# A message-passing layer: sums and counts leave PSUM on ScalarE and go to two tables in DRAM, in place of adds on VectorE, and 48 feature columns a step are copied on chip in place of 40

## The chip, the cores and the metric

The kernel runs on one core of a Trainium2 chip. The metric is the device time of one execution in microseconds (us). Before the change it is 1895.83 us, the median of three runs (1894.88 to 1898.73).

A core has TensorE (PE: matmuls out of SBUF into PSUM), VectorE (DVE), ScalarE (ACT), GpSimd (POOL) and SyncE (SP), each with an instruction queue of its own, and 16 DMA engines that all queues share. SBUF and PSUM are the memories on the chip, of 128 partitions each; DRAM is off it.

## The reference, cut to what matters

`x` holds 12,500 nodes with 64 features. There are 212,500 edges with 32 features each, sorted by their destination, and every node has at least the edge from itself.

```
msg_in   = concat(x[src], x[dst], edge_attr)              # 160 values an edge
messages = relu(msg_in @ mW1 + mb1) @ mW2 + mb2           # 160 -> 128 -> 64
agg      = segment_sum(messages, dst)                     # one row a node
u        = relu(concat(x, agg) @ uW1 + ub1) @ uW2 + ub2   # 128 -> 128 -> 64
out      = layernorm(x + u)                               # over 64 values, no gain
```

The second message product is linear, so it can follow the sum. The kernel sums the 128 hidden values of a node's edges, counts the edges (for `mb2`), and multiplies the sums once by `wc` = mW2 @ uW1[64:].

## The kernel before

**Groups and steps.** The edges form 554 groups of `GE` = 384 (three tiles of 128). Since they are sorted, the destinations of a group lie in a window of `W` = 32 nodes. One step `k` of the main loop (lines 716 to 772) works on three groups at once: `turn` on group k, `hidden` on k-2, `sums` on k-4. In the last ten steps (`SHORT`) the three catch up with each other.

- `turn` (line 423): `own.s` holds an edge a row: 64 gathered source features, and a one-hot of 32 columns for its destination within the window, which VectorE writes (`onehot`, line 409). TensorE transposes the three tiles into PSUM, and ScalarE copies the result, 96 rows by 384, to `own.st` (line 440).
- `hidden` (line 448): one matmul a tile, of `own.st` (64 rows source features, 32 rows one-hot, 32 rows edge features that a DMA has put there) with `own.wm` (64 rows of mW1, the window's 32 rows of `by_dst`, which is x @ mW1[64:128] + mb1 in DRAM, and 32 rows of mW1). VectorE takes the relu to `own.h` (line 464).
- `sums` (line 474): one matmul a tile of the hidden values with the one-hot (the one-hot four times side by side, `TIMES`), 128 hidden by 32 nodes, and one of ones with the one-hot for the counts. VectorE adds the sums to `agg` (128 by nodes in SBUF, line 493) and the counts to row 96 of `xc` (line 494), at columns that come from a register which `places` has loaded.

**Where source features come from.** For most groups POOL gathers them: an indirect DMA a tile (line 184), 16 groups ahead, into a ring of 20. Beside that, the transposed features of all nodes lie in SBUF as `xc`. For the groups in `COPIED` there is no gather: VectorE (line 597) and ScalarE (line 599) copy single columns of `xc`, 64 partitions by four bytes, into `own.st`, at addresses that they load into registers first (line 576). From step `BEGIN` = 18 on, `COLS` = 40 columns go each step, 20 on each of the two engines, in parts of `VCOLS` and `ACOLS`. Once 384 are done another group is complete; 54 groups are copied in this way.

**The update of nodes.** Nodes go in 25 chunks of 512. A chunk is closed at a group whose number follows from the edges' count (`PLAN`); from then on one part of its update runs in each step (`step_update`, line 663): `inner` (two products of 512 columns), `relu`, `outer` (eight products), `stats`, `root`, `scaled` with the store of the output.

**Order.** Each engine runs its instructions in the order written. A step's matmuls wait once, at the first, for all that the step needs; PSUM has two slots for each of the three parts, so a step waits for the copies, relus and adds of two steps earlier. SP's queue holds in program order the window loads (`window`, line 390, four groups ahead), the edge features (`inputs`, line 355), the indices and the outputs. A second program, `unordered`, runs only if a test on the chip finds that the edges do not fit.

## Time and profile before

| what | value |
|---|---|
| median of three runs | 1895.83 us |
| the profiled execution | 1894.96 us, its span 1893.1 us |
| mean granted TensorE clock | 0.963 |
| busy: PE, DVE, ACT, POOL | 1336.2, 1475.6, 1385.6, 1418.0 us |
| indirect gathers on POOL | 1499, 945 ns each |
| column copies on ACT and on DVE | 10360 and 10376 |
| moved by DMA | 104.90 MB, 55 GB/s on average |

Busy time is time in which an engine executes; loads of registers, semaphore operations and the issue of DMAs do not count as busy. A row of a group reads: line, engine, operation, output and inputs, count, then busy time in all and mean ns of one, then the idle time of the engine just before such instructions and what ended most of it. The profile infers who ended a wait from semaphore events, so a name there can be wrong where several things had been waited for. Timelines give start and length in us from the start of the span; an fp32 matmul appears as two instructions.

### The profile page before, as it was taken

The page shows a single profiled execution, that of the slowest core. Times are in us where ns is not written, and L with a number is a line of the kernel's source. Part 1 is how long each engine was busy: PE and PEld are TensorE (multiplying, and loading weights), DVE is VectorE, ACT ScalarE, POOL GpSimd, SP SyncE. Part 2 cuts the span into 40 slices and gives each one's busy share as a digit, 9 for nine tenths or more (in the row PEclk, how much of TensorE's full clock was granted, in tenths as well). Part 3 has the DMA queues.
Part 4 walks back from the last instruction along what each step waited for, and adds up shares of the span by engine and source line. Part 5 has one row for each costly group of instructions (what it writes and reads, how often), then busy time and mean ns, then how long its engine had stood idle before and what let it go on. Part 6 is the DMA issues. An engine that isn't in the chain of part 4 may idle for free. (4 is left out here: it accounts for less than half of the span.)

```text
span 1893.1 us, 60001 instructions
## 1 busy us (share of the span) xinstructions
PE 1336.2 (71%) x12323; PEld 1182.5 (62%) x12323; DVE 1475.6 (78%) x13054; ACT 1385.6 (73%) x11008; POOL 1418.0 (75%) x1506
## 2 busy tenths in 40 slices
PE   5877777757667666777677766776766757666767
PEld 4766666656556555666566665666666656656666
DVE  4468898878878788778887887878878888788763
ACT  3368888877777777777787777777777877777741
POOL 7777777777777777777777777777777777777774
PEclk9789999999999999989998999999999999999998
DMA  5542222222222222222222222222222222222221
GB/s 144 138 98 64 54 51 53 48 51 48 45 53 53 46 52 48 50 49 50 49 53 46 52 45 53 53 46 53 48 51 48 48 51 53 45 54 48 50 48 28
DMA packets 113382, 104.90 MB, mean 55 GB/s; under 512 B 51873, under 2 KB 83246, under 8 KB 113006
## 3 DMA queue, kind: packets, MB, share of 16 engines
q0 software_dynamic: 47968, 49.19, 13.6%
q1 hardware_dynamic: 64194, 51.30, 10.0%
q14 instruction: 272, 2.23, 0.4%
q8 instruction: 104, 1.70, 0.4%
q10 hardware_dynamic: 844, 0.48, 0.1%
HBM read 91.19 MB, written 9.62 MB: 53 GB/s over the span
## 5 line engine op out<-in xcount | busy, mean ns | idle before, releaser
L184 POOL DMA_INDIRECT own_s<-in_x,src_sb x1499 | 1417.3, 945 | 457.9 <-DMA own_s<-in_x,src_sb 206.3
L599 ACT ACTIVATE own_st<-own_xc 64x4 uint8 x10360 | 1089.2, 191 | 66.7 <-issue 18.6
L597 DVE COPY own_st<-own_xc 64x4 uint8 x10376 | 894.5, 191 | 171.1 <-issue 146.9
L429 PE MATMUL own_ps<-own_ident,own_s 128*96 128x128 f32 x1661 | 292.4, 287 | 512.0 <-ACT own_st L599 230.9
L440 ACT ACTIVATE own_st<-own_ps 96x384 f32<-96x384 f32 (+1 forms) x554 | 267.3, 483 | 383.0 <-PE own_ps L486 341.6
L429 PEld LDWEIGHTS own_ps<-own_ident,own_s 128*96 128x96 f32 x1661 | 166.4, 130 | 572.8 <-ACT own_st L599 311.4
L481 PE MATMUL own_ps<-own_s,own_h 128*128 128x128 f32 x3322 | 483.7, 284 | 1.9 <-DVE own_h L464 1.3
L453 PE MATMUL own_ps<-own_wm,own_st 128*128 128x128 f32 x3322 | 479.9, 283 | 0.0
L481 PEld LDWEIGHTS own_ps<-own_s,own_h 128*128 128x128 f32 x3322 | 436.0, 200 | 3.8 <-DVE own_h L464 2.4
L464 DVE TENSOR_SCALAR own_h<-own_ps 128x384 f32<-128x384 f32 x553 | 303.1, 548 | 167.4 <-PE own_ps L486 152.3
L453 PEld LDWEIGHTS own_ps<-own_wm,own_st 128*128 128x128 f32 x3322 | 431.7, 198 | 1.4 <-issue 0.5
L486 PE MATMUL own_ps<-own_s,own_one 128*1 128x32 f32 x3322 | 190.0, 194 | 0.0
L486 PEld LDWEIGHTS own_ps<-own_s,own_one 128*1 128x1 f32 x3322 | 114.5, 84 | 70.1 <-issue 7.2
L412 DVE TENSOR_TENSOR own_s<-iota,dlc 128x96 f32<-128x96 f32 x554 | 135.7, 246 | 0.8
L494 DVE TENSOR_TENSOR own_xc<-own_ps,own_xc 1x32 f32 x554 | 102.0, 184 | 28.8 <-PE u_ps L505 11.0
L493 DVE TENSOR_TENSOR own_agg<-own_ps,own_agg 128x32 f32 x554 | 97.9, 177 | 18.1 <-PE own_ps L486 10.3
L383 PE MATMUL u_ps<-w1b,own_xc 65*128 65x128 f32 x196 | 33.9, 325 | 28.6 <-DMA own_xc<-in_xT 12.6
L383 PEld LDWEIGHTS u_ps<-w1b,own_xc 65*128 65x128 f32 x196 | 28.7, 225 | 31.3 <-issue 20.3
L517 PE MATMUL u_ps<-same,own_xc 65*128 65x64 f32 (+1 forms) x196 | 39.5, 284 | 0.5 <-ACT u L510 0.5
L386 ACT ACTIVATE t<-u_ps 128x512 f32<-128x512 f32 (+1 forms) x25 | 14.7, 587 | 33.4 <-DMA by_dst<-t 16.7
L519 PE MATMUL u_ps<-u,u 128*128 128x64 f32 (+1 forms) x196 | 38.3, 277 | 0.0
L517 PEld LDWEIGHTS u_ps<-same,own_xc 65*128 65x128 f32 (+1 forms) x196 | 29.9, 192 | 2.4 <-ACT u L510 0.8
(60 smaller groups left out, 262.1 us busy)
## 6 DMA issues: line engine op xcount, KB each, us to landing
own_st<-in_efT SPq DMA_DIRECT2D x138, 192.0 KB
own_s<-in_x,src_sb POOLq DMA_INDIRECT x1499
own_wm<-by_dst SPq DMA_DIRECT2D x554, 16.0 KB
by_dst<-t SPq DMA_DIRECT2D x24, 256.0 KB
out<-o SPq DMA_DIRECT2D x24, 128.0 KB
own_xc<-in_xT SPq DMA_DIRECT2D x12, 179.2 KB
index<-in_src_copied SPq DMA_DIRECT2D x64, 1.2 KB
dlc_i<-in_dst_cols SPq DMA_DIRECT2D x1, 807.0 KB
```

Source lines behind the costliest of these rows:

```text
L184: nc.gpsimd.indirect_dma_start(out=s[:p, j, :D], out_offset=None, in_=x[:, :], in_offset=bass.IndirectOffsetOnAxis(ap=src_sb[:p, g * TG + ...
L412: places_by[g] = nc.vector.tensor_tensor(own.s[g % RING][:, :, D:], iota.unsqueeze(1).to_broadcast([P, TG, W]), dlc[:, g * TG : (g + 1) * ...
L429: nc.tensor.transpose(xt[:, j * P : j * P + p], sides[g] if g in sides and j == TG - 1 else s[:p, j, :], ident[:p, :p])
L440: after(nc.scalar.activation(t[r, c : c + n], xt[r, :n], AF.Copy), step))]
L453: nc.tensor.matmul(pre[:p, j, :], t[:, c + j * P : c + j * P + p], wm[g % NW], start=True, stop=True)
L464: relu_by[g] = [nc.vector.tensor_scalar(h, pre, 0.0, None, ALU.max)]
L481: did.append(nc.tensor.matmul(sg, h[:p, j, :], s[:p, j, D:].unsqueeze(1).to_broadcast([p, TIMES, W]), start=j == 0, stop=j == len(sizes) - 1))
L486: did.append(nc.tensor.matmul(counted, own.one[:p], s[:p, j, D:], start=j == 0, stop=j == len(sizes) - 1))
L493: a = after(nc.vector.tensor_tensor(agg[:, at], sg[:, 0, :], agg[:, at], ALU.add), step)
L494: return [a, after(nc.vector.tensor_tensor(count, counted, count, ALU.add), step)]
L597: by[engine] = nc.vector.tensor_copy(o, x_at)
L599: by[engine] = nc.scalar.activation(o, x_at, AF.Copy)
```

## The change

- `sums` now has the one-hot as the weights and the hidden values as the moving operand: the result is 32 nodes by 128, the counts are one column beside it. They lie in the same PSUM tile as the transposes of the step, at rows 64 to 95 and columns 384 to 512. ScalarE's copy of a step takes them along: 513 columns instead of 384. The adds on VectorE, their register loads (`places`) and `agg` are gone.
- SP stores the 32 rows, with 32 rows of zeros behind them, from `own.st` to a table in DRAM, even groups to one and odd groups to the other, at the window's first node (`store`). In the same table a later group overwrites the zeros of an earlier one, and at most two groups, one of each table, share a node.
- The update of a chunk begins two steps later (`SETTLED`) and has twelve parts in place of six: `found` loads the chunk's rows of both tables, `settled` only lets a step pass, `counts` and `all_sums` transpose and add the two by matmuls with the identity, `count_moved` (ScalarE) and `moved` (VectorE) copy the results out of PSUM; `inner` has three products.
- `hidden` runs three steps behind `turn` instead of two, `sums` six instead of four.
- `VCOLS` and `ACOLS` have another part of four each: 48 columns a step. A column is copied as one float and no more as four bytes.
- The edge features of four groups are loaded as four pieces a row, as the sums' columns lie between them. The test on the chip also asks that windows start in rising order and that the zeros reach the next group of the same table. `unordered` takes other memory.

```diff
-NW = 2 * SB
-COUNT = 96
-NH = 3
+NW = 8
+SLOTS = 2
+TO_HIDDEN, TO_SUMS = 3, 6
+NH = TO_SUMS - TO_HIDDEN + 1
+PLACE = TG * P + 132
+ROW = H + 1
+STORED = 2 * W
...
-TIMES = 4
+SETTLED = 2
 BEGIN = 18
 CHECKED = 8
-VCOLS = (12, 8)
-ACOLS = (8, 4, 4, 4)
+VCOLS = (12, 8, 4)
+ACOLS = (8, 4, 4, 4, 4)
 COLS = sum(VCOLS + ACOLS)
...
-        self.ps = [[on(f"own_ps{i}{k}", P, 512, of=nc.psum_tensor) for k in range(3)]
-                   for i in range(2)]
+
+        self.ps = [on(f"own_ps{i}", P, 1024, of=nc.psum_tensor) for i in range(SLOTS)]
+        self.pre = [on(f"own_pre{i}", P, 512, of=nc.psum_tensor) for i in range(SLOTS)]
...
+    def zeroed():
+
+        for ps in own.ps:
+            nc.vector.memset(ps[:D, GE : GE + ROW], 0.0)
+        for t in own.st:
+            nc.vector.memset(
+                t[D + W :, :].rearrange("p (g c) -> p g c", g=SB)[:, :, GE : GE + ROW], 0.0)
+        for n in range(0, STORED, W):
+            nc.sync.dma_start(tables[1][n : n + W, :], own.st[0][D + W :, GE : GE + ROW])
...
+    tables = [dram.tile([NP + STORED, ROW], F32, name=f"by_node{i}") for i in range(2)]
...
-        efs_by[b] = nc.sync.dma_start(own.st[b % BLOCKS][D + W :, : c1 - c0], a["efT"][:, c0:c1])
-        after(efs_by[b], *([hidden_by[(b - BLOCKS + 1) * SB - 1]] if b >= BLOCKS else []))
+        t = own.st[b % BLOCKS][D + W :, :].rearrange("p (g c) -> p g c", g=SB)
+        n, rest_n = divmod(c1 - c0, GE)
+        efs_by[b] = [nc.sync.dma_start(
+            t[:, :n, :GE], a["efT"][:, c0 : c0 + n * GE].rearrange("p (g c) -> p g c", g=n))]
+        if rest_n:
+            efs_by[b].append(nc.sync.dma_start(t[:, n, :rest_n], a["efT"][:, c0 + n * GE : c1]))
+        for i in efs_by[b]:
+            after(i, *([hidden_by[(b - BLOCKS + 1) * SB - 1]] if b >= BLOCKS else []))
...
+            for i in range(n):
+                at, store_at[g + i] = (of_words(v[2 * i + j].with_bounds(
+                    min_val=0, max_val=4 * size * (N - 1))) for j, size in enumerate((H, ROW)))
+                rows_at[g + i] = at
...
+    def store(g):
+
+        t, c, _ = columns(g + TO_SUMS)
+        table = tables[g % 2].rearrange("n w -> (n w)").bitcast(U8)
+        store_by[g] = nc.sync.dma_start(
+            table[bass.ds(store_at.pop(g), 4 * STORED * ROW)].rearrange("(n b) -> n b", n=STORED),
+            t[D:, c + GE : c + GE + ROW].bitcast(U8))
+        tc.add_to_no_dep_group("features", store_by[g].ins)
...
+            if step in with_sums:
+                n = GE + ROW
             copies = [ordered_by_steps(
-                after(nc.scalar.activation(t[r, c : c + n], xt[r, :n], AF.Copy), step))]
+                after(nc.scalar.activation(t[r, c : c + n], ps[r, :n], AF.Copy), step))]
...
-        sg = ps[2][:, : TIMES * W].rearrange("p (t w) -> p t w", w=W)
-        counted = ps[2][0:1, TIMES * W :][:, :W]
+        found, counted = ps[D : D + W, GE : GE + H], ps[D : D + W, GE + H : GE + ROW]
         did = []
-        for j, p in enumerate(sizes):
-            did.append(nc.tensor.matmul(
-                sg, h[:p, j, :],
-                s[:p, j, D:].unsqueeze(1).to_broadcast([p, TIMES, W]),
-                start=j == 0, stop=j == len(sizes) - 1))
-        for j, p in enumerate(sizes):
-            did.append(nc.tensor.matmul(counted, own.one[:p], s[:p, j, D:],
-                                        start=j == 0, stop=j == len(sizes) - 1))
-
-        def add(step):
+        for out_ps, of in ((counted, lambda j, p: own.one[:p]), (found, lambda j, p: h[:p, j, :])):
+            for j, p in enumerate(sizes):
+                did.append(nc.tensor.matmul(out_ps, s[:p, j, D:], of(j, p), start=j == 0,
+                                            stop=j == len(sizes) - 1))
+        emptied = store_by.get(g - BLOCKS * SB)
+
+        def moved(step):
             sums_by[g] = step
-            at = bass.ds(starts.pop(g), W)
-            count = xc[COUNT : COUNT + 1, at]
-            a = after(nc.vector.tensor_tensor(agg[:, at], sg[:, 0, :], agg[:, at], ALU.add), step)
-            return [a, after(nc.vector.tensor_tensor(count, counted, count, ALU.add), step)]
-
-        return did, [*relu_by[g], *copy_by[g]], add
+            if step in with_sums:
+                return copy_by[g + TO_SUMS]
+            t, c, _ = columns(g + TO_SUMS)
+            r = slice(D, D + W)
+            return [after(nc.scalar.activation(t[r, c + GE : c + GE + ROW], ps[r, GE : GE + ROW],
+                                               AF.Copy), step)]
+
+        return did, [*relu_by[g], *copy_by[g], *([emptied] if emptied else [])], moved
 
     def update(base, p, n):
 
         rows, q = slice(base, base + p * n), p * n
 
-        def inner():
+        def found():
+            parts = [found_p.tile([P, 4, ROW], F32, name=f"found{i}") for i in range(2)]
+            for t, table in zip(parts, tables):
+                nc.sync.dma_start(t[:p, :n], table[rows, :].rearrange("(n p) w -> p n w", p=p))
+            return parts
+
+        def settled(parts):
+            return parts
+
+        def joined(parts, w, rows_out):
+            ps = ups.tile([H, CH], F32, name="u_ps")[:rows_out]
+            for k in range(n):
+                for i, t in enumerate(parts):
+                    nc.tensor.matmul(ps[:, k * p : (k + 1) * p], t[:p, k, w], ident[:p, :p],
+                                     start=i == 0, stop=i == 1)
+            return ps
+
+        def counts(parts):
+            return parts, joined(parts, slice(H, ROW), 1)
+
+        def count_moved(got):
+            parts, ps = got
+            count = up.tile([1, CH], F32, name="count")
+            nc.scalar.activation(count[:, :q], ps[:, :q], AF.Copy)
+            return parts, count
+
+        def all_sums(got):
+            parts, count = got
+            return joined(parts, slice(0, H), H), count
+
+        def moved(got):
+            ps, count = got
+            agg = up.tile([H, CH], F32, name="agg")
+            nc.vector.tensor_copy(agg[:, :q], ps[:, :q])
+            return agg, count
+
+        def inner(moved_to):
+            agg, count = moved_to
             u_ps = ups.tile([H, CH], F32, name="u_ps")
-            nc.tensor.matmul(u_ps[:, :q], wc, agg[:, rows], start=True, stop=False)
-            nc.tensor.matmul(u_ps[:, :q], ux, xc[: COUNT + 1, rows], start=False, stop=True)
+            nc.tensor.matmul(u_ps[:, :q], wc, agg[:, :q], start=True, stop=False)
+            nc.tensor.matmul(u_ps[:, :q], per_edge, count[:, :q], start=False, stop=False)
+            nc.tensor.matmul(u_ps[:, :q], ux, xc[: D + 1, rows], start=False, stop=True)
...
-        return [inner, relu, outer, stats, root, scaled]
+        return [found, settled, counts, count_moved, all_sums, moved, inner, relu, outer, stats, root, scaled]
...
-            o = t.bitcast(U8)[:D, 4 * (first_c + c) : 4 * (first_c + c + 1)]
-            x_at = xc_bytes[:D, bass.ds(at - own.at, 4)]
+            o = t[:D, first_c + c : first_c + c + 1]
+            x_at = xc_bytes[:D, bass.ds(at - own.at, 4)].bitcast(F32)
...
-        if not now and waiting and waiting[0][0] <= g:
+        if not now and waiting and waiting[0][0] + SETTLED <= g:
...
-            ps, old = own.ps[g % 2], users[part][g % 2]
+            slot = (g + ahead_of[part]) % SLOTS
+            ps, old = (own.pre if part is hidden else own.ps)[slot], users[part][slot]
...
+        if {turn, sums} <= {part for part, _ in work}:
+            with_sums.add(did[-1])
         for part, g, _, _, follow in parts:
-            users[part][g % 2] = follow(did[-1])
+            users[part][(g + ahead_of[part]) % SLOTS] = follow(did[-1])
+        unstored.extend(g for part, g in work if part is sums)
+
+    def stored():
+
+        while unstored:
+            store(unstored.pop(0))
...
-            if k + 2 < BITS:
-                zeroed(k + 2)
...
-        if k % SB == 1:
-            places(k // SB + 1)
         if k < G - SHORT:
-            step((turn, k), *([(hidden, k - 2)] if k > 1 else []),
-                 *([(sums, k - 4)] if k > 3 else []))
-            made, summed = max(0, k - 1), max(0, k - 3)
+            step((turn, k), *([(hidden, k - TO_HIDDEN)] if k >= TO_HIDDEN else []),
+                 *([(sums, k - TO_SUMS)] if k >= TO_SUMS else []))
+            made, summed = max(0, k + 1 - TO_HIDDEN), max(0, k + 1 - TO_SUMS)
...
+        stored()
...
-        step_update(G)
+        step_update(G + SETTLED)
+    return sums_by[G - 1]
```

## The prediction

> **What bounds the kernel now.** I read the page's busy table first, then the costliest groups, the waits of GpSimd (POOL), its timeline at both ends, and a table of stretches. Busy shares alone decide nothing: four engines stand between 71% and 78%.

> ```profile
> span 1893.1 us, 60001 instructions
> PE 1336.2 (71%) x12323; PEld 1182.5 (62%) x12323; DVE 1475.6 (78%) x13054; ACT 1385.6 (73%) x11008; POOL 1418.0 (75%) x1506
> ...
> L184 POOL DMA_INDIRECT own_s<-in_x,src_sb x1499 | 1417.3, 945 | 457.9 <-DMA own_s<-in_x,src_sb 206.3
> L599 ACT ACTIVATE own_st<-own_xc 64x4 uint8 x10360 | 1089.2, 191 | 66.7 <-issue 18.6
> L597 DVE COPY own_st<-own_xc 64x4 uint8 x10376 | 894.5, 191 | 171.1 <-issue 146.9
> ```

> The 458 us that POOL sits idle look like slack. Its waits and the two ends of its timeline say otherwise:

> ```profile
> POOL own_s L184 <- DMA own_s<-in_x,src_sb: 206.3, 677, 0.3
> POOL own_s L184 <- issue: 196.0, 643, 0.3
> POOL own_s L184 <- ACT own_st L599: 37.5, 123, 0.3
> ```
> ```profile
> 2.96 1.15 POOL L184 DMA_INDIRECT own_s<-in_x,src_sb  x1 [1.38 <-DMA src_sb<-in_src]
> ...
> 1874.65 0.94 POOL L184 DMA_INDIRECT own_s<-in_x,src_sb  x1 [0.30 <-issue]
> 1875.89 0.89 POOL L184 DMA_INDIRECT own_s<-in_x,src_sb  x1 [0.30 <-issue]
> ```

> Every idle piece is 0.3 us (206.3/677, 196.0/643), whatever name it carries, and none is longer. So a gather costs 0.945 + 0.305 = 1.25 us, always: (1875.89 - 2.96)/1498 = 1.2503 us from first to last. POOL never waits for anybody; it is full, and its last gather starts 17.2 us before the span's end. The other engines follow it, as the pace of TensorE's (PE's) transposes shows (line 429, three matmuls to a step; columns: stretch, length, PE busy and count, weight loads):

> ```profile
> 180.00:280.00 100.00, 17.16 (x102) 9.79 (x102) 1.00 0.23 53
> ...
> 600.00:1000.00 400.00, 62.54 (x356) 35.28 (x357) 0.97 0.23 51
> ```

> Early, while gathered groups are still in store, 102/3 = 34 steps take 100 us, 2.94 us each; later 356/3 = 118.7 steps take 400 us, 3.37 each, and POOL's own is 1499 x 1.2503/554 = 3.383. PE, ScalarE (ACT) and VectorE (DVE) could thus go some 13% faster than they are fed.

> **What the change takes from POOL.** A column-copied group needs no gather. 40 columns a step make 54 such groups, 48 make 65: with starts at step 18 the formula gives ceil(384(n+1)/48) steps more for each, up to group 538. Gathers: 1499 - 11 x 3 = 1466. Worth 33 x 1.2503 = **41.3 us**. POOL's need falls to 1466 x 1.2503/554 = 3.308 us a step.

> **Can the others follow at 3.308?** ScalarE is the one to ask. While it ran at its own speed:

> ```profile
> 187.58 2.09 ACT L599 ACTIVATE own_st<-own_xc 64x4 uint8 x20
> 188.41 0.83 PE L481 MATMUL own_ps<-own_s,own_h 128*128 128x128 f32 x6
> 189.57 0.47 ACT L440 ACTIVATE own_st<-own_ps 96x384 f32<-96x384 f32 x1
> 190.17 2.09 ACT L599 ACTIVATE own_st<-own_xc 64x4 uint8 x20
> 192.16 0.47 ACT L440 ACTIVATE own_st<-own_ps 96x384 f32<-96x384 f32 x1
> ```

> From copy to copy 192.16 - 189.57 = 2.59 us with 20 columns, one every (2.09 - 0.19)/19 = 0.10 us. Four more add 0.40. The copy out of PSUM grows from 384 to 513 columns; two rows give the price of a column:

> ```profile
> L386 ACT ACTIVATE t<-u_ps 128x512 f32<-128x512 f32 x24 | 14.3, 596 | 31.4 <-PE u_ps L383 16.3 <-DMA by_dst<-t 14.7
> L440 ACT ACTIVATE own_st<-own_ps 96x384 f32<-96x384 f32 x499 | 241.0, 483 | 369.3 <-PE own_ps L486 330.9 <-PE own_ps L429 25.2 <-issue 9.3
> ```

> (596 - 483)/128 x 129 = 114 ns, of which part lies under the register load that separates copy and first column already (0.60 us from 189.57 to 190.17); between 0 and 0.11 I take 0.05. Each chunk of the update (one in about 22 steps) adds a count copy of 512 columns, 0.6/22 = 0.03, to a relu and a root that were there (0.04). Together 3.1 us a step: below 3.308, by 6%. That margin is the thin place of the forecast.

> VectorE loses the two adds and gains four columns:

> ```profile
> L494 DVE TENSOR_TENSOR own_xc<-own_ps,own_xc 1x32 f32 x554 | 102.0, 184 | 28.8 <-PE u_ps L505 11.0
> L493 DVE TENSOR_TENSOR own_agg<-own_ps,own_agg 128x32 f32 x554 | 97.9, 177 | 18.1 <-PE own_ps L486 10.3
> ```

> -199.9 us against 2104 x 894.5/10376 = +181, and 25 copies of 512 columns out of PSUM, +15 at 0.6 each (ScalarE's row, DVE has none of this size): 1472 us, 2.66 a step. The register load of every fourth step for the adds goes too. Not a bound.

> PE keeps its six sum matmuls, with a 32-column weight in place of 128; no row has that form, so between -0.4 us a step (half of the 0.83 above) and 0; I take 0, as the long move of 128 columns stays. The update gets 392 more matmuls against the identity (eight a chunk for counts, eight for sums) at 0.83/3 = 0.277, and a third product: 392 x 0.277 + 25 x 1.0 = 134 us, or 0.24 a step on PE's 1336.2/554 = 2.41 busy. Hidden in mid-kernel.

> SyncE issues one more transfer a step, 64 rows of 516 bytes, and two table loads a chunk, 31 MB in all beside 105 MB moved now. Its store waits for ScalarE's copy of the same step; behind it stand the window loads (needed seven steps after the one that issues them), edge features and indices. The loads of a chunk wait for the last stores:

> ```profile
> SPq L402 <- DMA by_dst<-t: 49.2, 23, 3.7
> ```

> A load behind a write of DRAM waited 49.2/23 = 2.1 us here; such a wait once in 22 steps is covered by those seven. If that cover failed, 25 x 2.1 = 53 us would be the most it could cost PE. I take 0.

> **The end is where the change pays back.** Nothing covers what follows the last gather. These rows are the end of before:

> ```profile
> 1859.42 1.13 PE L504 MATMUL u_ps<-own_agg,wc 128*128 128x512 f32 x2
> 1860.38 1.02 PE L505 MATMUL u_ps<-own_xc,ux 97*128 97x512 f32 x2
> ...
> 1866.57 0.43 PE L517 MATMUL u_ps<-same,own_xc 65*128 65x64 f32 x2
> ...
> 1868.18 0.39 PE L519 MATMUL u_ps<-u,u 128*128 128x64 f32 x2
> ...
> 1869.81 0.22 DVE L526 BATCH_NORM_STATS2 stats<-u_ps 128x6 f32<-128x64 f32 x1
> ...
> 1871.06 0.18 DVE L527 BATCH_NORM_AGGREGATE mv<-stats 128x2 f32<-128x6 f32 x1
> ...
> 1873.19 0.28 ACT L533 ACTIVATE rstd<-mv,eps 128x4 f32<-128x4 f32 x1
> ...
> 1875.35 0.18 DVE L538 RECIPROCAL rstd<-rstd 128x4 f32<-128x4 f32 x1
> 1875.57 1.10 DVE L541 TENSOR_SCALAR o<-u_ps,mv,rstd 128x64 f32<-128x64 f32 x4
> 1876.69 0.41 SPq L546 DMA_DIRECT2D out<-o  x1
> ...
> 1882.78 0.62 PE L504 MATMUL u_ps<-own_agg,wc 128*128 128x212 f32 x2 [0.28 <-DVE own_agg L493]
> 1883.86 0.35 ACT L510 ACTIVATE u<-u_ps 128x212 f32<-128x212 f32 x1 [4.81 <-PE u_ps L505]
> ```

> The last chunk but one ran its six parts beside the last steps, from 1859.42 to 1876.69; the last chunk began at 1882.78, after the last sums. Now a chunk has twelve parts, one for each sums step, and begins two steps later. By the plan's closing groups (546 for the last but one) it begins at sums 548; when sums 553 are done six parts are over, and inner, relu, outer, stats, root and scaled follow with nothing beside them. Only then, in program order on SyncE behind that chunk's output, come the last chunk's loads. New on the path, in us:
> - its joined sums (8 x 0.277 = 2.2) between the last steps on PE, and its counts two steps ahead, mostly in PE's idle time: 2.5 (0 to 4);
> - inner 3.0 (1859.42 to 1861.40 is 2.0 for two products, a third of 512 columns 1.0); relu 0.7 (596 ns and the handover); outer 2.0 (1866.57 to 1868.57); stats 1.5 (1869.81 to 1871.24); root 0.4; reciprocal and scaled 1.4; the output's issue 0.5: 9.5;
> - two loads, the second issued 0.4 later and landing 2.1 after: 2.5. For a load's landing the nearest is the index load that the first gather waits for, issued at 0.81 and followed by the gather at 2.96; twice that is the upper bound;
> - counts of the last chunk (4 x 0.277 and handovers, 1.2), their copy 0.4, sums 1.2, their copy 0.5: 3.3;
> - the third product of its inner part 0.5.

> ```profile
> 0.81 0.42 SPq L151 DMA_DIRECT2D src_sb<-in_src  x1
> ```

> Sum **18.3 us**, between 14 and 24. The last store (0.3 copy, issue, 2.1) ends under the 9.5 and costs nothing; without that cover it would cost 3. From the last relu on nothing changes.

> **Sum.** The profiled execution took 1894.96 us, 1.86 more than its span, and stands 0.9 under the median of the runs, 1895.83. 1894.96 - 41.3 + 18.3 = 1872.0.

> **The rivals.**
> *ScalarE becomes the bound* (the slower side). Its margin is 0.2 us a step; a column at 0.11 instead of 0.10, the whole 0.11 of the copy and a wait for late steps would use it up. For it: the 2.94 of the early stretch is 0.35 over the clean 2.59. Against it: part of that 0.35 were VectorE's register loads for the adds, which go. Copying lasts some 520 steps; at 3.40 a step it falls 520 x 0.092 = 48 us behind POOL, and the last 15 steps without copies, at about 2.6 against 3.75 for three gathers, give back 17: about 1872 + 31 = 1903. From about 3.38 a step on the gain is gone.

> *VectorE's copies hold POOL up.* The column copies turn from four bytes into one float. A long conversion did slow a gather:

> ```profile
> 22.01 1.00 DVE L263 CAST dlc<-dlc_i 128x1614 f32<-128x1614 int32 x1 [8.66 <-DMA dlc_i<-in_dst_cols]
> ...
> 22.39 1.44 POOL L184 DMA_INDIRECT own_s<-in_x,src_sb  x1 [0.30 <-issue]
> ```

> 1.44 instead of 0.94. But 10376 short copies beside 1499 gathers left their mean at 945 ns. A delay of 22.9/1466 = 0.016 us in every gather cancels the gain; 0.04 gives 1872 + 59 = 1931.
> [...]

> *The end stays as short as it was*: the chunks' new parts find room earlier, and the whole 41.3 comes through, 1853.7. The code's order speaks against it.

> **How the numbers follow.** Forecast 0.79, ScalarE 0.10, VectorE's copies 0.06, short end 0.05. The likeliest case's own range is 1894.96 - 41.3 + 14 to + 24, 1867 to 1878. The range for all reaches to 1862 and 1886: it takes in a lag of a few us that ScalarE has not made good when the copies end, and an end 5 us shorter than my lower bound. About 0.2% of this kernel, 3.8 us, can be told from no change. Faster: 0.79 + 0.05 = 0.84; the two slow cases give 0.05 to no change (a pace near 3.38, or a delay near 0.016) and 0.11 to slower.

> **What would show it.** 1466 gathers 1.25 us apart with idle pieces of 0.3 each, the last starting near 1834.6; ScalarE's group of column copies at 12480 and its busy time near 1685 (1385.6 + 2120 x 0.105 + 554 x 0.114 + 25 x 0.6); transposes at 2.94 to 3.2 us a step until about step 200 and 3.3 after; from the last gather's start to the span's end 35 us in place of 17.2, with the last chunk but one entirely behind the last sums. Wrong it would be if POOL's gathers show pieces over 0.3 that wait for ScalarE's copies, if their mean leaves 945 ns, or if transposes stay above 3.31 a step.

## The result and the profile after

The changed kernel takes **1879.83 us** (median of four runs, 1878.41 to 1880.89) where the kernel before takes 1895.36 beside it: a ratio of 0.9916, 95% interval 0.9899 to 0.9933. It is 15.5 us faster; 23.8 were forecast (1895.83 - 1872.0). The profiled execution took 1878.41 us, 1.72 more than its span of 1876.69.

The page of the changed kernel: span, busy time of each engine, then the three costliest groups.

```profile
span 1876.7 us, 66058 instructions
PE 1495.1 (80%) x13157; PEld 1217.2 (65%) x13157; DVE 1362.5 (73%) x14069; ACT 1619.6 (86%) x13169; POOL 1385.6 (74%) x1473
...
L193 POOL DMA_INDIRECT own_rows<-in_x,src_sb x1466 | 1384.8, 945 | 447.9 <-issue 178.6
L668 ACT ACTIVATE own_operands<-own_xc 64x1 f32 x12480 | 1295.1, 189 | 28.4 <-issue 6.7
L666 DVE COPY own_operands<-own_xc 64x1 f32 x12480 | 893.7, 136 | 283.4 <-issue 177.5
```

ScalarE is now the busiest engine, 86%. Whether it is the bound is read from POOL's waits (total, times, longest) and from the last gathers:

```profile
POOL own_rows L193 <- issue: 178.6, 586, 0.3
POOL own_rows L193 <- DMA own_rows<-in_x,src_sb: 132.3, 434, 0.3
POOL own_rows L193 <- ACT own_operands L668: 92.3, 303, 0.3
```

```profile
1832.13 0.95 POOL L193 DMA_INDIRECT own_rows<-in_x,src_sb  x1 [0.30 <-issue]
1833.38 0.90 POOL L193 DMA_INDIRECT own_rows<-in_x,src_sb  x1 [0.30 <-DMA own_rows<-in_x,src_sb]
```

Behind the first gather, which waits for its indices, no piece is over 0.3 us, whoever is named, as before. POOL is still full: 33 gathers fewer, and the last starts 42.5 us earlier (1875.89 to 1833.38). The pace of TensorE's transposes (three a step; stretch, length, TensorE's busy time and count, weight loads, granted clock) shows the other engines catching up and then following:

```profile
200.00:400.00 200.00, 33.73 (x195) 19.46 (x195) 0.98 0.34 71
400.00:600.00 200.00, 34.68 (x200) 19.41 (x198) 0.98 0.34 71
...
1400.00:1800.00 400.00, 65.62 (x366) 36.98 (x365) 0.94 0.33 68
```

65 steps in 200 us are 3.08 us each, then 3.0, and 3.28 at the end (366/3 = 122 steps in 400 us) where only POOL sets the pace: while columns are copied, one group in eight needs no gather (48/384), and 2.625 gathers a step at 1.25 us are 3.28. So at 48 columns the engines can go at about 3.05 and are fed at 3.28.

Of the 42.5 us, 26.05 come back behind the last gather: span minus its start is 1876.69 - 1833.38 = 43.31, against 1893.15 - 1875.89 = 17.26 before. The timeline of the end:

```profile
1842.32 1.13 PE L572 MATMUL u_ps<-agg,wc 128*128 128x512 f32 x2
...
1851.43 0.40 SPq L615 DMA_DIRECT2D out<-o  x1
1851.94 1.11 SPq L536 DMA_DIRECT2D found<-by_node  x2
1857.29 0.51 PE L546 MATMUL u_ps<-own_ident,found 106*1 106x106 f32 x2 [9.05 <-SPq L1155]
1859.91 1.22 PE L546 MATMUL u_ps<-own_ident,found 106*1 106x106 f32 x6 [2.11 <-SPq L1155]
...
1864.07 1.08 PE L572 MATMUL u_ps<-agg,wc 128*128 128x212 f32 x2 [0.47 <-DVE agg L566]
...
1867.18 0.35 ACT L579 ACTIVATE u<-u_ps 128x212 f32<-128x212 f32 x1 [5.68 <-PE u_ps L574]
```

The last chunk but one runs from `inner` at 1842.32 to its output at 1851.83 (1851.43 + 0.40); then the last chunk's two loads are issued, and it takes 8.0 us until the second has landed (1851.94 to 1859.91); in that time TensorE does 0.51 us of work, on the first load. The stretches of the same place (length, five engines' busy time, granted clock, DMA share, GB/s):

```profile
1854.00:1856.00 2.00, 0.00 (x0) 0.00 (x0) 0.00 (x0) 0.00 (x0) 0.00 (x0) 0.50 0.14 40
...
1864.00:1866.00 2.00, 1.93 (x4) 1.00 (x4) 0.01 (x1) 0.00 (x0) 0.00 (x0) 0.50 0.00 0
```

In the first nothing computes and the load uses 0.14 of 16 DMA engines, about two (0.14 x 16 = 2.2). In the second TensorE works at a granted clock of 0.50.

### The profile page after: what moved, and what is told of

The parts are those of the page before. It is cut to its first block, busy times and chain, and to the rows that moved or that the text cites. A ratio compares the mean times of both kernels' runs of the same rounds, so it can differ in the third digit from the quotient of the medians.

```text
span 1876.7 us, 66058 instructions
## 1 busy us (share of the span) xinstructions
PE 1495.1 (80%) x13157; PEld 1217.2 (65%) x13157; DVE 1362.5 (73%) x14069; ACT 1619.6 (86%) x13169; POOL 1385.6 (74%) x1473
## 5 line engine op out<-in xcount | busy, mean ns | idle before, releaser
L193 POOL DMA_INDIRECT own_rows<-in_x,src_sb x1466 | 1384.8, 945 | 447.9 <-issue 178.6
L668 ACT ACTIVATE own_operands<-own_xc 64x1 f32 x12480 | 1295.1, 189 | 28.4 <-issue 6.7
L666 DVE COPY own_operands<-own_xc 64x1 f32 x12480 | 893.7, 136 | 283.4 <-issue 177.5
L456 PE MATMUL own_ps<-own_ident,own_rows 128*96 128x128 f32 x1661 | 299.2, 292 | 302.6 <-ACT own_operands L668 109.6
L482 PE MATMUL own_pre<-own_wm,own_operands 128*128 128x128 f32 x3322 | 492.4, 288 | 0.0
L514 PE MATMUL own_ps<-own_h,own_rows 128*32 128x128 f32 x3322 | 482.3, 284 | 0.0
L482 PEld LDWEIGHTS own_pre<-own_wm,own_operands 128*128 128x128 f32 x3322 | 444.3, 203 | 2.4 <-issue 1.6
L469 ACT ACTIVATE own_operands<-own_ps 96x513 f32<-96x513 f32 (+2 forms) x554 | 321.8, 581 | 129.5 <-PE own_ps L514 108.0
L493 DVE TENSOR_SCALAR own_h<-own_pre 128x384 f32<-128x384 f32 x553 | 300.1, 543 | 172.4 <-PE own_ps L514 134.7
L514 PEld LDWEIGHTS own_ps<-own_h,own_rows 128*32 128x32 f32 x3322 | 336.6, 116 | 6.0 <-issue 0.2
L546 PE MATMUL u_ps<-own_ident,found 128*1 128x128 f32 (+2 forms) x784 | 110.6, 298 | 19.8 <-SPq L1155 11.2
L546 PEld LDWEIGHTS u_ps<-own_ident,found 128*1 128x1 f32 (+2 forms) x784 | 80.8, 144 | 39.4 <-issue 16.7
L397 PE MATMUL u_ps<-w1b,own_xc 65*128 65x128 f32 x196 | 34.8, 332 | 39.8 <-DMA own_xc<-in_xT 15.5
```

The lines of the kernel that those rows point to most:

```text
L193: nc.gpsimd.indirect_dma_start(out=s[:p, j, :D], out_offset=None, in_=x[:, :], in_offset=bass.IndirectOffsetOnAxis(ap=src_sb[:p, g * TG + ...
L397: nc.tensor.matmul(ps[:, j], xc[: D + 1, base + j * P :][:, :P], w1b, start=True, stop=True)
L456: nc.tensor.transpose(xt[:, j * P : j * P + p], sides[g] if g in sides and j == TG - 1 else s[:p, j, :], ident[:p, :p])
L469: after(nc.scalar.activation(t[r, c : c + n], ps[r, :n], AF.Copy), step))]
L482: nc.tensor.matmul(pre[:p, j, :], t[:, c + j * P : c + j * P + p], wm[g % NW], start=True, stop=True)
L493: relu_by[g] = [nc.vector.tensor_scalar(h, pre, 0.0, None, ALU.max)]
```

## The experiments

**The parts apart.** The changed kernel with 40 columns, and the kernel before with 48.

```diff
-VCOLS = (12, 8, 4)
-ACOLS = (8, 4, 4, 4, 4)
+VCOLS = (12, 8)
+ACOLS = (8, 4, 4, 4)
```

> The changed kernel with 40 columns a step again (VectorE 12+8, ScalarE 8+4+4+4), all else as changed. Theory (GpSimd's 1.25 us a gather sets the middle, the longer end is the price): 1499 gathers, the last at about 1876, then the same 43 us to the end: 1921 us, some 41 above the changed kernel and 26 above the kernel before. Rival (the gain comes from the adds that left VectorE, not from the gathers): well under 1895. Rival (ScalarE's late steps make the end long): the end shrinks to some 35 us, about 1913.

Measured 1922.78 us (1920.33 to 1923.29), ratio 1.0146 (1.0129 to 1.0163). The page: 1499 gathers again.

```profile
L193 POOL DMA_INDIRECT own_rows<-in_x,src_sb x1499 | 1416.7, 945 | 458.0 <-issue 205.8
```

The last gather starts at 1875.43, 0.5 from where it did before, and 45.7 us follow it. So the change without its added columns costs 27.7 us (1922.78 - 1895.09), all of it at the end, and the 48 columns on top of it bring 42.9 (1922.78 - 1879.83).

The reverse edit, the first pair of lines for the second, in the kernel before:

> The kernel before with 48 columns a step alone; sums are still added on VectorE. If GpSimd stays the bound: 1466 gathers, the last at about 1834, the old end of 17 us: 1854 us, better than the changed kernel. Rival (VectorE, with adds and 24 columns, becomes the bound: 2.94 us a step in the early stretch plus four columns at 0.086, 3.28, plus waits for registers): transposes about 3.3 us or more apart to the end, 1865 to 1900.

Measured **1971.7 us** (1964.13 to 1973.62), ratio 1.0399 (1.0374 to 1.0425): outside the times of both theories, though the rival named the right engine. The same 33 gathers fewer now lose 77 us. Its transposes stand at 3.45 us a step (348/3 = 116 steps in 400 us), its page has VectorE at 84%, and its waits:

```profile
600.00:1000.00 400.00, 59.72 (x348) 33.75 (x346) 0.98 0.23 48
```

```profile
PE own_ps L429 <- ACT own_st L440: 421.3, 325, 2.8
...
POOL own_s L184 <- ACT own_st L440: 114.6, 172, 4.6
```

POOL is blocked for up to 4.6 us here: it no longer sets the pace. The waits of TensorE name ScalarE's copy (L440). The waits of VectorE itself, from 600 to 1000, put the delay elsewhere:

```profile
DVE own_st L597 <- issue: 38.8, 130, 0.6
...
DVE own_h L464 <- PE own_ps L486: 0.2, 1, 0.2
```

In these 400 us VectorE waits for another engine once, for 0.2 us; the rest of its idle time is "issue", in which it waits for nothing that the profile shows, as while it loads addresses into registers (1560 loads in this run, 0.60 us each in the median). So VectorE sets the pace here. The timeline of one step fits:

```profile
1204.52 0.55 DVE L464 TENSOR_SCALAR own_h<-own_ps 128x384 f32<-128x384 f32 x1
...
1205.19 0.18 DVE L494 TENSOR_TENSOR own_xc<-own_ps,own_xc 1x32 f32 x1
1205.48 0.50 PE L429 MATMUL own_ps<-own_ident,own_s 128*96 128x128 f32 x3 [1.54 <-ACT own_st L440]
...
1207.67 0.54 DVE L464 TENSOR_SCALAR own_h<-own_ps 128x384 f32<-128x384 f32 x1
...
1208.34 0.18 DVE L494 TENSOR_TENSOR own_xc<-own_ps,own_xc 1x32 f32 x1
1208.63 0.51 PE L429 MATMUL own_ps<-own_ident,own_s 128*96 128x128 f32 x3 [1.04 <-ACT own_st L440]
```

Twice the next step's transposes begin 0.11 us after VectorE's second add has ended (1205.37 and 1208.52), and VectorE goes from relu to relu in 3.15 us, with the two adds in that distance. The step waits for several semaphores; the name in the row is one of them, and the add looks like the last, which is read from the times and not shown otherwise. In the changed kernel, where the adds are gone, the same distance is 2.83:

```profile
371.41 0.54 DVE L493 TENSOR_SCALAR own_h<-own_pre 128x384 f32<-128x384 f32 x1
...
374.24 0.54 DVE L493 TENSOR_SCALAR own_h<-own_pre 128x384 f32<-128x384 f32 x1
```

**Form and depth.** Either of two smaller parts could have made that room: copies as one float, and layers further apart.

```diff
-            o = t[:D, first_c + c : first_c + c + 1]
-            x_at = xc_bytes[:D, bass.ds(at - own.at, 4)].bitcast(F32)
+            o = t.bitcast(U8)[:D, 4 * (first_c + c) : 4 * (first_c + c + 1)]
+            x_at = xc_bytes[:D, bass.ds(at - own.at, 4)]
```

> The changed kernel with its column copies written as four bytes each, as in the kernel before, and not as one float. If POOL sets the pace (my theory): the same 1466 gathers of 945 ns, 1880 us, within 3 us of the changed kernel. If it was the shorter float copies that made room on VectorE (rival): VectorE gets 12480 copies of about 86 ns busy in place of 72, some 175 us more over 390 steps or 0.45 us a step, so its clean step goes from about 2.85 to about 3.3, it stands at POOL's 3.31, and with the table loads and the products of the updates above it: 1890 to 1930 us.

Measured 1881.34 us (1879.47 to 1883.36), ratio 0.9933 (0.9916 to 0.995). The page:

```profile
L193 POOL DMA_INDIRECT own_rows<-in_x,src_sb x1466 | 1385.5, 945 | 448.0 <-issue 183.5
L666 DVE COPY own_operands<-own_xc 64x4 uint8 x12480 | 1079.3, 189 | 157.6 <-issue 139.5
```

VectorE's copies cost 1079.3/12480 = 86 ns in place of 893.7/12480 = 72, 186 us more in all, and its idle time ahead of them falls by 126. Nothing of it reaches the end; the rival falls. While catching up, VectorE goes from relu to relu in 2.84 us in this run too (301.99 to 304.83).

```diff
-TO_HIDDEN, TO_SUMS = 3, 6
+TO_HIDDEN, TO_SUMS = 2, 4
```

> The changed kernel with the layers 2 and 4 steps behind, as in the kernel before, and not 3 and 6. If the pace is POOL's and the depth gives only slack (my theory): 1880 us, or 2 to 5 us less, since the last sums then come two steps earlier behind the last gather. If the depth is needed to keep ScalarE and VectorE from waiting for one another (rival): steps of 3.4 to 3.5 us and 1900 us or more.

Measured 1881.28 us (1880.03 to 1881.39), ratio 0.993 (0.9914 to 0.9947): the same as the changed kernel. The depth is not needed, and two steps less bring nothing at the end either (44.3 us behind the last gather). With form and depth out, each by itself, the missing adds remain as what lets VectorE carry 48 columns. No run puts the adds alone back, but the sizes fit: with byte copies a clean step takes 2.84 us without the adds and 3.15 with them, and the two adds are 0.17 and 0.18.

**The end.** First the width of the last chunk's loads: its 212 nodes lie as two loads of 106 partitions; here they are four of 112.

```diff
-                nc.sync.dma_start(t[:p, :n], table[rows, :].rearrange("(n p) w -> p n w", p=p))
+            wide = -(-p // 16) * 16
+                for k in range(n):
+                    nc.sync.dma_start(t[:wide, k], table[base + k * p : base + k * p + wide, :])
```

> The changed kernel; only the last chunk's loads differ: four of 112 partitions in place of two of 106 (six rows more than needed). Theory (106 rows go through two DMA engines, which makes 8.0 us from first issue to the last product's start): 4 us instead of 8, time about 1876. Rival (the 8 us are latency of DRAM or a wait for the last store): no change, 1880.

Measured 1876.25 us (1874.7 to 1877.99), ratio 0.9902 (0.9885 to 0.9918); this overlaps the changed kernel's interval, and the trace has to decide. Its timeline:

```profile
1856.38 1.84 SPq L541 DMA_DIRECT2D found<-by_node  x4
1858.45 0.51 PE L551 MATMUL u_ps<-own_ident,found 106*1 106x106 f32 x2 [5.78 <-DMA found<-by_node]
1859.47 1.22 PE L551 MATMUL u_ps<-own_ident,found 106*1 106x106 f32 x6 [0.50 <-DMA found<-by_node]
```

3.1 us from the first issue to the last load's use, against 8.0, with twice as many loads. In the profiled execution little of that reaches the end: the span is 1876.19 against 1876.69. Its last gather starts 1.0 us later (1834.42), and TensorE's clock halves earlier, so that the chunk before the last takes 12.5 us (1843.76 to 1856.26) in place of 9.5. The DMA share is 0.39 from 1858 to 1860 here, 89 GB/s, against the 0.14 and 40 GB/s above. The changed kernel's records of single transfers fit the 0.14: each of its two loads of 106 ends with 2 writes of four bytes (1856.40 and 1856.66, 1859.07 and 1859.36), the store of the output ahead of them with 16 (1852.92 to 1853.06). So the loads of 106 ran on about two engines and those of 112 on more; whether the width or the split into four brought that is not shown, as no run has four loads of 106.

Then the place of the loads: as they are, but issued right behind the last store and not after the chunk before is done.

```diff
+    ready = waiting[-1][1][0]()
+    waiting[-1][1][0] = lambda: ready
     while now or waiting:
         step_update(G + SETTLED)
```

> The changed kernel; only the last chunk's loads are issued right behind the last store, ahead of the rest of the chunk before it. Theory: the 8.0 us lie under the 9.5 us of that chunk, 1872 us; if TensorE's clock also stays up, since its pause gets shorter, 2 us less still, 1870. Rival (the loads are not what the end waits for): 1880.

Measured **1872.34 us** (1871.9 to 1872.98), ratio 0.9884 (0.9867 to 0.99), as expected. Its timeline:

```profile
1843.84 1.54 SPq L536 DMA_DIRECT2D found<-by_node  x2
...
1853.58 0.41 SPq L615 DMA_DIRECT2D out<-o  x1
1853.61 1.57 PE L546 MATMUL u_ps<-own_ident,found 106*1 106x106 f32 x8 [3.21 <-DVE o L610]
```

The slow loads lie under the chunk before; the last counts begin 6.3 us earlier (1859.91 to 1853.61). The clock fell all the same, and earlier, at about 1846.6, where TensorE had paused for no more than 0.69 us. In the kernel with the wide loads it fell in a stretch in which TensorE was busy throughout, so no long pause is needed to halve it (first row: early loads, second row: wide loads):

```profile
1846.00:1848.00 2.00, 1.31 (x7) 1.28 (x7) 0.00 (x0) 0.60 (x1) 0.00 (x0) 0.66 0.10 23
```

```profile
1844.00:1846.00 2.00, 2.00 (x4) 0.35 (x3) 0.00 (x0) 0.19 (x1) 0.00 (x0) 0.86 0.07 17
```

Last, both edits and, in the last steps, two parts of an update in each step:

```diff
+            if g > PLAN[-2][3] + SETTLED:
+                step_update(g)
```

> The kernel of the early loads, with the last chunk's loads as four of 112 partitions, and with two parts of an update in place of one in each of the last steps, so that the chunk before the last is nearly done when the last sums are stored. If the rest of that chunk (9.5 us) delays the end: it goes under the last steps, and the last chunk starts on its loads, 1866 to 1869 us beside 1872. If the last store and the landing of the loads set the end with or without it (rival): 1871 to 1873 us.

Measured 1871.35 us (1870.94 to 1872.44), ratio 0.9875 (0.9859 to 0.9892): 1 us under the one before, inside the scatter of both. The parts did move: the last loads are issued at 1849.22 and used at 1852.00, but 1849.22 follows the last sums' copy (1848.34) and its store, which came 5.4 us later than in the kernel with the early loads (1842.96). What was taken from the end was put ahead of the last sums; the rival holds.

**More columns.** If POOL is full and the others have room, more copies should pay. 56 columns, 28 on each engine, with the early loads:

```diff
-VCOLS = (12, 8, 4)
-ACOLS = (8, 4, 4, 4, 4)
+VCOLS = (12, 8, 8)
+ACOLS = (8, 4, 4, 4, 8)
```

> The kernel of the early loads with 56 copied columns (28 and 28): 76 copied groups, 1433 gathers, 3.23 us of POOL a step. If POOL still set the pace: 33 x 1.25 = 41 us less than 1872, 1831 us. My theory is that VectorE and ScalarE then set it: 2.85 clean plus four copies on each (about 0.4) plus 0.25 for updates is 3.5 us a step, some 0.2 over the changed kernel's 3.31 in 400 steps, so 1900 us or more.

Measured 1988.82 us (1983.2 to 1991.86), ratio 1.0488 (1.0466 to 1.051): slower, as expected. Its transposes go at 3.48 us a step (345/3 = 115 in 400 us), and POOL is blocked for up to 5.6:

```profile
1000.00:1400.00 400.00, 60.51 (x345) 34.74 (x345) 0.97 0.32 64
```

```profile
POOL own_rows L193 <- issue: 243.3, 794, 0.8
POOL own_rows L193 <- ACT own_operands L469: 166.9, 199, 5.6
```

52 columns as 26 and 26, `VCOLS = (12, 8, 6)` and `ACOLS = (8, 4, 4, 4, 6)`:

> The kernel of the early loads with 52 copied columns a large group in place of 48 (26 by VectorE, 26 by ScalarE): 71 copied groups, 1448 gathers, 18 fewer. If POOL still sets the pace: 18 x 1.25 = 22 us less than 1872, 1850 us. If VectorE and ScalarE are already near their bound (rival): two more copies for each on a clean step of 2.85 us make about 3.05, the updates come on top with about 0.25, and 3.3 us stands at POOL's 3.27: no gain or a loss, 1865 to 1885 us.

Measured **3856.14 us** (3842.79 to 3863.72), twice as long, where neither theory had anything like it. Its waits:

```profile
ACT own_operands L668 <- issue: 1823.7, 2617, 1.6
```

ScalarE stands still 2617 times for 0.70 us ahead of its column copies, five times a step, 3.5 us of 7.0. What precedes them are register loads of the columns' addresses, by line in the changed kernel and in this one (minimum, median, maximum in ns):

```profile
L645 ACTq TENSOR_LOAD <-index x2600: 305/311/981, 102.8 to 1787.7; - x186
```

```profile
L645 ACTq TENSOR_LOAD <-index x2620: 894/917/2289, 103.4 to 3792.8; - x188
```

Behind VectorE's 26 addresses all of ScalarE's loads begin two values past a multiple of four. The next run keeps 52 columns and takes that away: 28 and 24, `VCOLS = (12, 8, 8)` and `ACOLS = (8, 4, 4, 4, 4)`.

> The kernel of the early loads with 52 copied columns a group again, now 28 by VectorE (12, 8, 8) and 24 by ScalarE (8 and four times 4), so that each load of registers begins at a multiple of four values in its row, which all of ScalarE's did not in the split of 26 and 26. If the place in the row was the cause there (my theory): ScalarE's loads of four take 0.31 us again and not 0.91, ScalarE is as in the changed kernel (3.08 us of work and loads a step of 3.28), VectorE comes to 3.12 us a step as in the run with 56 columns, both below POOL's 3.27, and the 18 gathers fewer give up to 22 us: 1850 to 1862. If 52 columns themselves are the cause (rival): 7 us a step as there, 3800 us. If VectorE's 3.12 busy with its waits is the bound: 3.3 us a step or more, 1872 us or above.

Measured 1992.96 us (1986.82 to 1998.92), ratio 1.0526 (1.0508 to 1.0543). The loads did return:

```profile
L645 ACTq TENSOR_LOAD <-index x2620: 304/311/959, 102.2 to 1917.1; - x188
```

With 56 columns, where ScalarE copies 28 and all loads begin at a multiple of four, they take 0.31 us too (304/312/1128). So neither 52 columns nor more than 24 of them on ScalarE made the loads slow. What sets the run with 26 and 26 apart from both others is the place in the row, and as far as these runs can tell that was the cause of the 3856. But the gain I expected did not come. VectorE, with four columns more than in the changed kernel, goes from relu to relu in 3.21 us, and the gap of 0.35 stands ahead of eight copies whose addresses are loaded just before them (VectorE's loads take 0.60 us in this run, the median):

```profile
1000.56 0.54 DVE L493 TENSOR_SCALAR own_h<-own_pre 128x384 f32<-128x384 f32 x1
...
1003.27 0.57 DVE L666 COPY own_operands<-own_xc 64x1 f32 x8 [0.35 <-issue]
1003.77 0.54 DVE L493 TENSOR_SCALAR own_h<-own_pre 128x384 f32<-128x384 f32 x1
```

The changed kernel has 2.83 here and a pace of 3.08 when it catches up, 0.25 more for what the updates add; 3.21 + 0.25 = 3.46 is about this run's pace, 3.45, and above POOL's 3.27. I had taken the mean busy share, 3.12 us a step, for VectorE's need. Its waits from 600 to 1000 have one row, and no other engine in it:

```profile
DVE own_operands L666 <- issue: 66.3, 234, 0.7
```

With 28 columns on VectorE it makes no difference whether ScalarE copies 24 or 28: 3.45 us a step here, 3.48 with 56 columns. VectorE is thus at its limit somewhere between 24 and 28 columns.

> Both together, 52 columns as 28 and 24 and the two parts a step at the end. If the two gains are of different stages, they add: the run with 52 columns less what two parts a step gave, 1845 to 1858 us. If VectorE and ScalarE have no room left for the updates at 52 columns, two parts at once at the end give nothing more than the run with 52 columns.

Measured 1991.87 us (1988.92 to 1994.51), ratio 1.0513 (1.0495 to 1.053): the same as the run before; two parts a step gave nothing more.

The reverse split, 24 on VectorE and 28 on ScalarE, was to show ScalarE's own limit:

> The kernel of the early loads with 52 copied columns a group as 24 by VectorE and 28 by ScalarE (8, 4, 4, 4, 8), every load of registers at a multiple of four: VectorE as in the changed kernel (2.81 us of work and loads a step), ScalarE as in the run with 56 columns (3.32 us a step with the updates), POOL 3.27. My theory: ScalarE is the bound as soon as it has four columns more, the pace is 3.35 to 3.45 us and the time 1890 to 1960. Rival: at 52 only VectorE was short, ScalarE follows at 3.27, and the 18 gathers fewer show: 1850 to 1865 us.

Measured 2657.87 us (2652.37 to 2659.06), but on a chip where the kernel before took 2535.95, a third more than anywhere else; ratio 1.0468 (1.0444 to 1.0492). Its waits have a row that no other run here shows:

```profile
DVE own_h L493 <- remote: 377.5, 126, 64.9
```

Something that the profile doesn't name holds VectorE up for as long as 64.9 us. It is slower than the kernel before there too; what ScalarE with 28 columns could do by itself stays open.

## Why the prediction was right, and where its sum was off

The direction, the range (1862 to 1886) and the mechanism hold; 1872.0 was 6.4 us short of the profiled execution's 1878.41.

- **POOL is the bound, 33 gathers are worth 41.3.** Right. The last one starts 42.5 us earlier, with 945 ns each and 0.3 between; the 1.2 us over come from the mean distance, (1833.38 - 2.94)/1465 = 1.2493 against 1.2503.
- **ScalarE can follow with 3.1 us a step.** Right: around 370 us into the span, with no update in between, its copy out of PSUM comes every 2.73 to 3.13 us, 2.91 on average (2.59 + 0.40 + 0.05 = 3.04 was worked out), and the pace while catching up is 3.0 to 3.1. Its busy time is 1619.6, not 1685.
- **"Not a bound" for VectorE.** Right for the kernel as changed, but the sum of busy time could not show it: the kernel before with 48 columns is busy for 84% and VectorE sets its pace, at 3.45 us; without the adds the engines can go at 3.05, 0.23 us below POOL's 3.28. And it is VectorE that ends this road at 28 columns. The total, 1362.5, is 110 below the 1472 of the sum, which had priced the copies as bytes. The run with byte copies has 1498.2, 26 above the sum (one reason is that the rows of the adds overlap those of their neighbours, so that the total falls by less than their 199.9: in the kernel before with 48 columns a step's first add begins at 1204.99, and the relu ahead of it ends at 1205.07); float copies then take 136 off. The time does not depend on that, 1881.34 against 1879.83.
- **VectorE's copies hold POOL up.** Not so: 12480 single-float copies beside 1466 gathers leave them at 945 ns, in this form and as bytes.
- **The end grows by 18.3.** Measured 26.05, above the bound of 24. Term by term: joined sums 2.05 (2.5 forecast); the chunk before the last 9.5 (9.5); **the two loads 8.0 (2.5)**; counts to the last relu 7.27 in place of before's 1.08, so 6.2 (3.8); after that 0.2 (0). The loads are the term that failed: I took the landing of another load, 2.1 us, and called twice that an upper bound, without asking how many DMA engines loads of 106 partitions would run on (about two, at a share of 0.14). Four loads of 112 took 3.1 in place of 8.0; issuing the two early saved 6.3. That the 9.5 came out to the tenth is partly luck: the clock fell only after that chunk's products, at about 1848.7; where it fell earlier the same parts took 11.2 us (early loads) and 12.5 (wide loads).
- The other 2.4 us lie in products that ran at a granted clock of 0.50, 1.08 us a pair where the kernel before took 0.62. I had priced them from rows at full clock. Why the clock falls when it does was not settled: the early loads took the long pause away and it fell between 1846 and 1848 regardless.
- **The last store lies under the 9.5 and costs nothing.** Right: issued early, the loads that wait for it ran while the chunk before still did.

Together: 23.0 forecast on the profiled execution, plus 1.2 at the gathers, less 7.75 at the end, plus 0.1 outside the span (1.81 before, 1.72 after), makes 16.55, and 16.55 were measured (1894.96 - 1878.41).

## What to carry to other kernels

When a change moves work behind the last item of the bounding engine, price that tail term by term, and price a load there by its shape and by how many DMA engines carry it (about two of 16 for 106 partitions here), not by another load's landing: here one term of 5.5 us and a halved clock ate a third of the gain, and two lines that issue the loads earlier gave 7.5 us back. An engine's busy total did not say what it could carry: in the kernel before with 48 columns VectorE set the pace while busy for 84%. The clean distance between two of its fixed instructions plus 0.25 for the updates came within 0.05 us of the pace in three runs: 3.40 for 3.45 (that kernel), 3.46 for 3.45 (28 and 24) and 3.48 for 3.48 (28 and 28, 1003.85 to 1007.08). Whether it waits for other engines at all says which one sets the pace (VectorE in that kernel: once in 400 us, for 0.2). Where a wait names one engine, look in the timeline at what ended just before the waiting instruction began.
